# Sorting the tokens of two groups by expert through memory in a four-layer cross-attention kernel

## The chip, the cores and the metric

One core of one Trainium2 chip runs the kernel. The metric is device time in microseconds of one execution, as the median over runs. The engines are TensorE (PE, with its weight loads PEld), VectorE (DVE), ScalarE (ACT), GpSimd (POOL) and SyncE (SP, which here only issues transfers). Every engine takes its own instructions in the order of its own program; the engines wait for each other by semaphores. ACT and POOL can issue transfers too. All data is fp32 but for masks.

## The reference

x is 16 sequences of 56 tokens with 256 channels, the context 16 x 1500 rows of 128. Four layers follow each other, each with attention to the context:

```python
x = _L0_xattn_ref(x, ctx_1024, ...)                  # one head, gate, norm
x = _L1_xattn_ref(x, ctx_1024, mask_BxS2_bk0, ...)   # 16 heads, then feed-forward
x = _L2_xattn_ref(x, ctx_1024, mask_BxS_ik0, ...)    # self, cross, two experts
x = _L3_xattn_ref(x, ctx_1024, mask_BxS2_bk0, ...)   # as L1
```

The third layer has two sets of weights ("vision" and "language"). A token belongs to the first if its type and the next token's type are 1. The end of that layer, which the change rewrites:

```python
vm = vm.at[:, :-1].set((tt[:, :-1] == 1) & (tt[:, 1:] == 1))
mi = rms_norm(hidden_states, ln_post_attn_w)
v_out = jax.nn.silu(mi @ v_gate) * (mi @ v_up) @ v_down
l_out = jax.nn.silu(mi @ l_gate) * (mi @ l_up) @ l_down
hidden_states = hidden_states + jnp.where(vm, v_out, l_out)
```

Gate and up are 256 x 688, down is 688 x 256.

## The kernel before

The 16 sequences are four groups of G = 4; a group has T = 224 tokens, held as two tiles of TP = 112 rows. `items` lists 16 pieces of work, k = 4 x layer + group. For each k, `program` (L1554) runs the attention of that piece (`att0`, `att13`, `att2`), and between its steps it draws pieces of other work from a generator `beside(k)` (L1580): the closing of the piece before (`post...`, called `follows`), and the preparation of the piece after (`pre...`, called `ahead`). Each `yield` ends one such piece; its number is its weight in us, and `pace` (L451) draws pieces until the weights reach a share for each attention step (`SHARES`, L1265, in the third layer). So PE's program is one interleaved list, and work that is not done when an attention ends is run before the next starts. When `k` runs, `line["closed"]` counts the attentions that are closed; a closing waits for it.

*First layer.* `load_pair(n)` (L630) loads the contexts of sequences 2n and 2n+1, and for n > 0 loads the first of the two also turned (channels on partitions), through SP. `turn_pair(n)` (L655) turns the other one by 12 products with the identity (L661), and copies the results from PSUM on ACT and DVE (L666). `scores_pair` (L676) starts after that, by a dependency on the last of these products.

*Second and fourth layer.* `pre13` makes queries, `att13` runs the attention in the short form (only the last 384 context rows count here; a test at the start, L1650 to L1663, finds from the mask which of two programs runs), and `post13` (L992) makes the output product with Wo, the sum, a layer norm, and the feed-forward with W1 and W2. Four weights of 1 MB each go through three buffers (`wpool`, tag w).

*Third layer.* `pre2` (L1133) is norm, self-attention and queries. `att2` (L1462) runs 24 pairs of context blocks for a group: `largest` (L1306, products L1315, maxima L1320 on DVE), `weights_pair` (L1344, products L1352 and L1361, exponentials L1366 on ACT, and running sums `all` on POOL, L1378), `sums_chunk` (L1383, L1391), `keys` and `values` for the sequences ahead (L1286, L1298), `own_sums` (L1409). Weights `pw` have three buffers. `close_group` (L1427) ends a group: product L1435, sum, and `begin_norm` (L326), which scales the rows on POOL (L332).

`post2(gi)` (L1508) is the part quoted of the reference. Each group runs both experts over all of its 224 tokens: the normed rows are turned (`rmsnorm_T`, L337; `to_T`, L264, product L270), and multiplied by the channel weights and by the mask vm or its complement (L360), so that a token of the other expert is a row of zeros. For each expert 6 slices of gate and up, each 2 x 2 products (L1524), then tanh form of silu on ACT, DVE and POOL (L1534), 12 products with down (L1542) and a sum into x (L1548). So a block is 24 + 12 products over 224 tokens, and there are 8 blocks. Each loads its weights through SP.

Of the kernel before, what the change touches and what calls it, by code (L numbers as in the profile page):

```python
# [9 lines left out]
F32 = mybir.dt.float32  # L10
# [12 lines left out]
G = 4  # L23
# [39 lines left out]
def tile_kernel(ctx: ExitStack, tc: tile.TileContext, a, layers=4, groups=NG):  # L63
# [13 lines left out]
    small = ctx.enter_context(tc.tile_pool(name="small", bufs=10))  # L77
    ps_s = ctx.enter_context(tc.tile_pool(name="ps_s", bufs=7, space=PSUM))
    ps_o = ctx.enter_context(tc.tile_pool(name="ps_o", bufs=1, space=PSUM))

# [125 lines left out]
    nc.vector.memset(half_less, -0.5)  # L206
    ones = const.tile([B, 1], F32, name="ones")
    nc.vector.memset(ones, 1.0)
    vm = const.tile([128, B, N], BF16, name="vm")
    nvm = const.tile([128, B, N], BF16, name="nvm")  # L210
    rope = const.tile([TP, 32], F32, name="rope")

    consts = {}

    def load_constants():

        w = wpool.tile([128, 2048], F32, tag="w", name="room")
        consts["room"] = w
        nc.sync.dma_start(w[:, : B * N].bitcast(I32), a["token_types"].to_broadcast([128, B * N]))
        nc.sync.dma_start(  # L220
            w[:N, B * N : B * N + N].bitcast(I32), a["positions"].to_broadcast([N, N])
        )
        nc.sync.dma_start(w[:PR, 1408 : 1408 + N], a["causal"])

    def fill_constants():
# [31 lines left out]
        )  # L257
        nc.vector.tensor_copy(rope, rp[:TP, :32])


# [64 lines left out]

    def begin_norm(w, gi):  # L326

        x = xs[gi]
        rstd = rms_rstd(x, nc.gpsimd)
        xn = xpool.tile([TP, NT, D], F32, tag="xn", bufs=3, name="xn")  # L330
        for i in range(NT):
            nc.gpsimd.tensor_scalar(  # L332
                xn[:, i, :], x[:, i, :], rstd[:, i : i + 1], None, ALU.mult
            )
        begun[w, gi] = xn

# [293 lines left out]
    def load_pair(n):  # L630
# [8 lines left out]
        for b, queue in ((2 * n, nc.sync), (2 * n + 1, other)):  # L639
# [10 lines left out]
            kvs.append(kv[:CP])  # L650
        if n:
            nc.sync.dma_start(kts[0], a["ctxT"][2 * n])
        halves_of[n] = kts, kvs

    def turn_pair(n):  # L655
        kts, kvs = halves_of[n]
        for s in range(NS):
            for i in range(1 if n else 0, 2):
                t = turn()
                for j in range(4):  # L660
                    last = nc.tensor.transpose(  # L661
                        t[:, j * CP : (j + 1) * CP], kvs[i][:, 4 * s + j, :], ident[:CP, :CP]
                    )
                dst = kts[i][:, s * SW : (s + 1) * SW]
                if (i + s) % 2:
                    nc.vector.tensor_copy(dst, t[:, :SW])  # L666
                else:
                    scalar_copy(dst, t[:, :SW])
        halves_of[n] = kts, kvs, last.ins.name

# [5 lines left out]
    def scores_pair(n):  # L676
# [7 lines left out]
        for s in range(NS):  # L684
            sc = psum(ps_s, "sc")
            cols = slice(s * SW, (s + 1) * SW)
            for i in range(2):
                product = nc.tensor.matmul(
                    sc[i * 64 : (i + 1) * 64, :SW], qT[:, b0 + i, :], kts[i][:, cols],
                    start=True, stop=True,  # L690
                )

                tc.add_manual_dep(
                    product.ins, turned_at,
                    mybir.DependencyInfo(
                        mybir.DependencyClass.NoSync, mybir.DependencyReason.DATA
                    ),
                    reason="products in halves stand together",
                )
            nc.vector.tensor_scalar(  # L700
# [290 lines left out]

    def post13(name, gi, state, some=range(NT)):  # L992
        x = xs[gi]
        oT = state["oT"]
        gc = GATE[name + "_attn"]
        if "wo" not in state:
            (state["wo"],) = load_w((a[name + "_Wo"], 8, D))
            (state["w1"],) = load_w((a[name + "_W1"], 2, FFI))
        wo, w1 = state["wo"], state["w1"]
        yield  # L1000
# [17 lines left out]

        yield from turned_back([oT[:, :, i * TP : (i + 1) * TP] for i in some], wo, gc)
        if "w2" not in state:  # L1020
            (state["w2"],) = load_w((a[name + "_W2"], 8, D))
        w2 = state["w2"]
        xT = yield from layernorm_T(gi, name + "_ln_ff_g", name + "_ln_ff_b", some)
# [240 lines left out]
    PAIRS = NC // 2  # L1264
    SHARES = 1.9, 2.4, 2.4, 1.5  # L1265

# [160 lines left out]
    def close_group(b):  # L1427

        if b % G == G - 1:
# [10 lines left out]
            line["closed"] += 1  # L1440
            begin_norm("L2_ln_post_attn_w", b // G)

# [19 lines left out]
    def att2(gi, state, then, ends):  # L1462

        for k in range(G):
            b = gi * G + k
            for j in range(PAIRS):
# [6 lines left out]
                weights_pair(b, j)  # L1473
                pace(SHARES[gi], -0.8, 1)
                last, n = (b, 2 * j - 2) if j else (b - 1, NC - 2)
# [31 lines left out]

    def post2(gi, state):  # L1508
        x = xs[gi]
        xf = x.rearrange("p i d -> p (i d)")  # L1510

        wg, wu = (load_w((a[f"L2_v_{w}"], 2, I2))[0] for w in ("gate", "up"))
        xe = yield from rmsnorm_T("L2_ln_post_attn_w", gi, True)
        yield
        for n, e in enumerate("vl"):
            (down,) = load_w((a[f"L2_{e}_down"], NF2, D))
            hT = big.tile([128, 8, T], F32, tag="hT", bufs=2, name="h2T")
            for f in range(NF2):
# [3 lines left out]
                for k, wt in enumerate((wg, wu)):  # L1522
                    for c in range(2):
                        nc.tensor.matmul(  # L1524
                            p[:w, k * T : (k + 1) * T], wt[:, c, cols], xe[n][:, c, :],
                            start=(c == 0), stop=(c == 1),
# [8 lines left out]
                yield 1.6  # L1535
            if e == "v":
                wg, wu = (load_w((a[f"L2_l_{w}"], 2, I2))[0] for w in ("gate", "up"))
            p = mm()
            for i in range(NT):
                for f in range(NF2):  # L1540
# [5 lines left out]
                    if f % 3 == 2 and i + f < NF2:  # L1546
                        yield 1.3
            nc.vector.tensor_add(xf, xf, p[:TP, : NT * D])  # L1548
            yield 1.3

    def program():  # L1554
        line.update(turn=None, sum=None, side=iter(()), rate=1, closed=0, pair=None, due=0.0, share=0.0)
        for kept in (memory_w, halves_of, queries, heads_w, cross, held, begun):
# [3 lines left out]
        for name in ("L1", "L3"):  # L1560
            parts.append(tuple(partial(f, name) for f in (pre13, first13, att13, post13)))
        parts.insert(2, (pre2, first2, att2, post2))
        items = [(*parts[l], gi) for l in range(layers) for gi in range(groups)]
# [16 lines left out]
        def beside(k):  # L1580
# [10 lines left out]
            if k + 1 < groups:  # L1591
                yield next(ahead)
            if k:
                _, _, _, post, gi = items[k - 1]
                follows = post(gi, states.get(k - 1))
            if k > groups:
                for work in ahead:
                    if isinstance(work, tuple):
                        while line["closed"] < k:
                            yield  # L1600
                        for _ in range(work[1]):
                            yield next(follows)
                    else:
                        yield work
            if k:
                while line["closed"] < k:
# [15 lines left out]
            if k + 1 == len(items) and short:  # L1622
                while line["pair"] != ("L3", groups - 1, 0):
                    yield
                yield from ending(k, 0)

        def ending(k, i):

# [3 lines left out]
            nc.sync.dma_start(a["out"][at : at + TP, :], xs[gi][:, i])  # L1632

        run(before(-1))
        first(0)
        for k, (_, _, att, _, gi) in enumerate(items):
            line.update(side=beside(k), share=1.8 if k + 1 == 2 * groups else 0.0)
            att(gi, states[k], partial(first, k + 1), gi == groups - 1)
            if k + 1 < len(items):
                run(line["side"])  # L1640
# [8 lines left out]

    mk = mpool.tile([B, M], U8, tag="own", bufs=1, name="mk")  # L1650
    nc.sync.dma_start(mk, a["mask"])
    lets = few(3)[:B]
    nc.vector.tensor_reduce(lets[:, 0:1], mk[:, : M - LW], AX.X, ALU.max)
    nc.vector.tensor_reduce(lets[:, 1:2], mk[:, M - LW :], AX.X, ALU.max)
    nc.vector.tensor_tensor(lets[:, 2:3], lets[:, 1:2], lets[:, 0:1], ALU.is_gt)
    load_x(0)
    nc.sync.dma_start(tables, a["tables"])
    t = turn()
    nc.tensor.matmul(t[:1, :1], lets[:, 2:3], ones, start=True, stop=True)
    only_last = const.tile([1, 1], I32, name="only_last")  # L1660
    nc.vector.tensor_scalar(only_last, t[:1, :1], float(B), None, ALU.is_equal)
    short = True
# [39 lines left out]
def layout(i):  # L1702
# [3 lines left out]
    def stacked(w):  # L1706
# [19 lines left out]
        ).view(np.uint32),  # L1726
        "mask": i["mask_BxS2_bk0"].view(np.uint8),
        "mask_last": np.ascontiguousarray(i["mask_BxS2_bk0"][:, M - LW :]).view(np.uint32),
# [16 lines left out]
    for l in ("L1", "L3"):  # L1745
# [3 lines left out]
        out[f"{l}_Wv"] = i[f"{l}_xattn_Wkv"][:, H * 64 :]  # L1749
    for w in (  # L1750
        "v_qkv", "l_qkv", "v_dense", "l_dense",
        "v_gate", "v_up", "v_down", "l_gate", "l_up", "l_down",
    ):
        out[f"L2_{w}"] = stacked(i[f"L2_xattn_{w}"])
    ckv = i["L2_xattn_ckv_w"]
    cd = i["L2_xattn_cdense_w"]
# [41 lines left out]
```

## Time and profile before

| what | value |
|---|---|
| three runs | 1456.79, 1458.99, 1459.77 us; median 1458.99 |
| the profiled execution | 1451.74 us, its span 1449.9 us |
| busy PE, DVE, ACT, POOL | 1387.7, 791.7, 742.5, 510.6 us |
| mean granted TensorE clock | 0.988 |
| moved by transfers | 131.08 MB |
| stages by lines: first layer | to about 128 us |
| second, third, fourth layer | to about 434, 1117, 1450 us |

A line of the groups of instructions gives: source line, engine, operation, tile written <- tiles read, shapes and count, then busy time in us, mean ns of one, and the idle time of the engine just before such instructions with what ended it. A line of the waits gives: engine, tile, line <- what released it, then us in total, times, and the longest. Busy digits of the page are tenths in 40 slices of 36 us. A line of transfers gives: target <- source, queue, count, KB of one, and us from issue to landing.

### The profile page before, as it was taken

How to read it: one execution, taken by the hardware profiler on the slowest of the kernel's cores; microseconds unless marked ns; L12 is line 12 of the kernel's file. 1: busy time of each engine (PE TensorE's matmuls, PEld its weight loads, DVE VectorE, ACT ScalarE, POOL GpSimd, SP SyncE). 2: the span in 40 equal slices, each digit the busy share in tenths (PEclk: the TensorE clock that was granted, in tenths of full speed). 3: DMA queues.
4: the chain of work that ended last, by engine and by line, in shares of the span. 5: the costliest groups of instructions: out<-in, count | busy, mean ns of one | idle time of the engine just before them, and what ended most of it. 6: DMA issues, size and time to landing. Idle time of an engine off the chain costs nothing.

```text
span 1449.9 us, 32736 instructions
## 1 busy us (share of the span) xinstructions
PE 1387.7 (96%) x13816; PEld 965.3 (67%) x13816; DVE 791.7 (55%) x1802; ACT 742.5 (51%) x1713; POOL 510.6 (35%) x554
## 2 busy tenths in 40 slices
PE   6999999998998999999999999999999999999997
PEld 4677677775775556655666556666666777777776
DVE  5454755547346574457555575445546546554641
ACT  2334857665353353535444354444545656756661
POOL 0021001010010566676677667767872110000000
PEclk9999999999899999999999999999999999999999
DMA  7823233241231202110112001221103333334230
GB/s 283 316 84 140 66 116 117 89 143 30 90 119 48 80 23 82 58 42 23 64 61 102 23 21 64 84 90 45 46 29 118 112 125 116 123 99 139 89 106 10
DMA packets 34298, 131.08 MB, mean 90 GB/s; under 512 B 8013, under 2 KB 14429, under 8 KB 30045
## 3 DMA queue, kind: packets, MB, share of 16 engines
q1 hardware_dynamic: 32701, 122.59, 24.7%
q0 software_dynamic: 720, 3.93, 0.7%
q8 instruction: 111, 1.82, 0.5%
q10 hardware_dynamic: 720, 2.36, 0.4%
q14 instruction: 46, 0.38, 0.1%
HBM read 127.95 MB, written 0.92 MB: 89 GB/s over the span
## 4 chain that ended last, share of the span: by engine, by line
PE 79%; DVE 10%; ACT 6%; DMA 2%; POOL 1%; issue 1%; SPq 0%; DVEq 0%; ACTq 0%; POOLq 0%
PE sc L562 10%; PE sc L544 8%; PE sc L1009 7%; PE sc L1315 7%; PE sc L1524 5%; PE o L1391 5%; PE sc L1361 4%; PE sc L825 4%; PE sc L1542 3%; PE sc L1298 3%; PE sc L1286 3%; DVE mx L1320 3%; PE sc L1031 3%; PE sc L1352 2%; PE sc L1152 2%; PE sc L897 2%
## 5 line engine op out<-in xcount | busy, mean ns | idle before, releaser
L1378 POOL TENSOR_TENSOR all<-all,pw 125x448 f32<-125x448 f32 x300 | 341.1, 1148 | 132.3 <-ACT pw L1366 121.2
L1320 DVE TENSOR_REDUCE mx<-sc 112x1 f32<-112x500 f32 x384 | 233.3, 668 | 113.1 <-PE sc L1315 113.0
L1366 ACT ACTIVATE pw<-sc 125x448 f32<-125x448 f32 x384 | 177.7, 549 | 95.8 <-PE sc L1361 91.7
L551 ACT ACTIVATE p<-p,few 128x384 f32<-128x384 f32 x224 | 136.9, 612 | 88.1 <-DVE few L547 87.8
L544 PE MATMUL sc<-ktl,qa 128*128 128x384 f32 x448 | 177.8, 505 | 0.0
L547 DVE CUSTOM_DVE_ANT_0 p<-sc,mkl 128x384 f32<-128x384 f32 x224 | 121.6, 551 | 87.2 <-PE sc L544 81.6
L562 PE MATMUL sc<-p,kvl 32*128 32x224 f32 x2160 | 153.1, 356 | 5.1 <-DVE qa L858 3.7
L142 POOL TENSOR_SCALAR mkl<-m32l 128x384 bf16<-128x384 uint8 x32 | 16.4, 513 | 397.3 <-DVE few L547 355.5
L562 PEld LDWEIGHTS sc<-p,kvl 32*128 32x128 f32 x2160 | 138.8, 187 | 21.1 <-issue 8.5
L562 PE MATMUL o<-p,kvl 32*128 32x224 f32 x720 | 146.3, 355 | 0.0
L562 PEld LDWEIGHTS o<-p,kvl 32*128 32x128 f32 x720 | 132.4, 187 | 0.0
L1315 PE MATMUL sc<-ck,qs 32*112 32x500 f32 x768 | 129.0, 624 | 3.1 <-ACT ck L262 1.4
L262 ACT ACTIVATE p<-p,few 128x384 f32<-128x384 f32 x224 | 120.7, 611 | 5.9 <-DVE few L538 5.9
L581 DVE STREAM_TRANSPOSE p<-p 128x768 f32<-128x768 f32 (+1 forms) x96 | 102.6, 1094 | 17.6 <-ACT p L262 17.1
L544 PEld LDWEIGHTS sc<-ktl,qa 128*128 128x128 f32 x448 | 78.9, 191 | 36.2 <-issue 8.2
L262 ACT ACTIVATE ot<-sc 128x224 f32<-128x224 f32 x64 | 31.9, 606 | 137.1 <-PE o L562 87.8
L1361 PE MATMUL sc<-qs,ck 32*125 32x224 f32 x1536 | 93.9, 349 | 0.0
L1391 PEld LDWEIGHTS o<-pw,vc 125*32 125x32 f32 x1536 | 40.1, 109 | 80.5 <-issue 68.8
L1391 PE MATMUL o<-pw,vc 125*32 125x224 f32 x1536 | 92.6, 359 | 0.0
L279 POOL TENSOR_TENSOR stat<-stat,half_less 112x2 f32<-112x2 f32 (+1 forms) x33 | 23.0, 699 | 183.7 <-DVE stat L292 143.8
L1524 PE MATMUL sc<-xT,w 128*128 128x224 f32 (+1 forms) x384 | 82.5, 359 | 0.0
L938 DVE COPY ot<-sc 128x224 f32<-128x224 f32 x32 | 18.2, 570 | 110.9 <-PE o L562 97.3
(265 smaller groups left out, 2419.0 us busy)
## 6 DMA issues: line engine op xcount, KB each, us to landing
kvl<-in_ctx_last SPq DMA_DIRECT2D x30, 768.0 KB, 4.3
kt<-in_ctxT SPq DMA_DIRECT2D x23, 750.0 KB, 5.0
w<-in_L_W SPq DMA_DIRECT2D x16, 1024.0 KB, 4.9
w<-in_L_Wq SPq DMA_DIRECT2D x8, 1024.0 KB, 4.9
w<-in_L_Wo SPq DMA_DIRECT2D x8, 1024.0 KB, 4.8
ktl<-in_ctxT SPq DMA_DIRECT2D x32, 192.0 KB, 2.5
w<-in_L_v_qkv SPq DMA_DIRECT2D x4, 768.0 KB, 4.5
w<-in_L_l_qkv SPq DMA_DIRECT2D x4, 768.0 KB, 4.4
```

Of the source, the lines that this page charges most:

```text
L262: nc.scalar.activation(out, in_, AF.Copy, scale=scale)
L544: nc.tensor.matmul(sc[:, :LW], u["q"][:, i * 128 : (i + 1) * 128], u["kt"], start=True, stop=True)
L547: nc.vector.tensor_tensor_reduce(u["p"][:, i], sc[:, :LW], u["mask"], 1.0, -LOWEST, ALU.add, ALU.min, mn[:, i : i + 1],)
L551: nc.scalar.activation(u["p"][:, i], u["p"][:, i], AF.Exp, bias=mn[:, i : i + 1], scale=-1.0, accum_out=den[:, i : i + 1],)
L562: product = nc.tensor.matmul(o[g][:, : RB * BW], y["kv"][part, j, :], y["p"][part, :, j * BW : (j + 1) * BW], start=j == 0, stop=j == LB - ...
L1315: nc.tensor.matmul(banks[g][: 2 * N, :SW], made["q"][part, rows], made["k"][part, cols], start=True, stop=True,)
L1320: nc.vector.tensor_reduce(made["mx"][:, half * 4 + g, s : s + 1], banks[g][: 2 * N, :SW], AX.X, ALU.max)
L1361: nc.tensor.matmul(banks[g][:CP, c * QH : (c + 1) * QH], made["k"][part, at : at + CP], made["q"][part], start=False, stop=c == 1, skip_gr ...
L1366: nc.scalar.activation(p[:, :, g * QH : (g + 1) * QH], banks[g][:CP, : 2 * QH].rearrange("p (c n) -> p c n", c=2), AF.Exp,)
L1378: engine.tensor_tensor(made["all"][:, cols], made["all"][:, cols] if j else p[:, 0, cols], p[:, c, cols], ALU.add,)
L1391: nc.tensor.matmul(made["o"][part, :QH], made["v"][:, n, part], p[:, r * QH : (r + 1) * QH], start=n == 0, stop=n + 1 == NC, skip_group_ch ...
L1524: nc.tensor.matmul(p[:w, k * T : (k + 1) * T], wt[:, c, cols], xe[n][:, c, :], start=(c == 0), stop=(c == 1),)
```

## The change

The change has four parts.

1. *The closing of the third layer by pairs of groups.* `post2(pair)` handles two groups (448 tokens) as 3 blocks of 224 rows. `begin_norm(..., sort=True)` writes each scaled row by an indirect transfer, issued by POOL, to a row buffer in DRAM (`sorted_rows`, 672 rows, filled with zeros early on); the row's place comes from a running count: vision tokens from the front, the others from the back. Block v takes the vision weights, block l the language weights, and the middle block b those of the one of the two that has more than 224 tokens; its weights are gathered by an indirect transfer with an index for each partition (`choice`). Results go to a second buffer (`made_rows`) through ACT's queue, and come back by an indirect gather for each half of a group (`back`).
2. *Closings held back.* `post13` of the second layer's groups 2 and 3 pauses before its feed-forward, and goes on beside the third layer's groups 0 and 1 (`late`). Pair 0 is closed beside groups 2 and 3 of the third layer, pair 1 beside the fourth layer's group 0. Shares change.
3. *Contexts of sequence pairs 4 to 7* are both loaded turned; `turn_pair` does nothing for them.
4. *The test of the mask* runs on 128 partitions instead of 16.

```diff
+    dpool = ctx.enter_context(tc.tile_pool(name="rows", bufs=1, space=bass.MemoryType.DRAM))
...
+        cp = mm()
+        nc.tensor.matmul(cp[:TP, :8], first[:, :TP], is_v, start=True, stop=False)
+        nc.tensor.matmul(cp[:TP, :8], every[:, :TP], carry, start=False, stop=True)
+        nc.vector.tensor_add(index, cp[:TP, :8], less)
+        nc.vector.tensor_copy(place[:TP], index)
...
-    def begin_norm(w, gi):
+    def begin_norm(w, gi, sort=False):
...
-        begun[w, gi] = xn
+            if sort:
+                nc.gpsimd.indirect_dma_start(
+                    sorted_rows[gi // 2], bass.IndirectOffsetOnAxis(place_of(gi, i), 0),
+                    xn[:, i, :], None,
+                )
+        if not sort:
+            begun[w, gi] = xn
...
-        if n:
-            nc.sync.dma_start(kts[0], a["ctxT"][2 * n])
+        for i in range(0 if n == 0 else 1 if n < 4 else 2):
+            nc.sync.dma_start(kts[i], a["ctxT"][2 * n + i])
...
-            for i in range(1 if n else 0, 2):
+            for i in range(0 if n == 0 else 1 if n < 4 else 2, 2):
...
+        while pause and pause():
+            yield
...
-    SHARES = 1.9, 2.4, 2.4, 1.5
+    SHARES = (2.3, 1.5), (2.3, 0.8), (2.3, 1.7), (1.65, 1.65)
...
-    def post2(gi, state):
+    def post2(pair):
+        def weights(e, name, c, f):
+            if e != "b":
+                return load_w((a[f"L2_{name}"][128 * "vl".index(e) :][:128], c, f))[0]
+            w = wpool.tile([128, 2048], F32, tag="w", name="w")[:, : c * f]
+            nc.gpsimd.indirect_dma_start(
+                w, None, a[f"L2_{name}"],
+                bass.IndirectOffsetOnAxis(choice[:, pair : pair + 1], 0),
+            )
+            return w.rearrange("p (c f) -> p c f", c=c)
+        def rows_of(n):
+            rows = tmp("rows")[:TP].rearrange("p (i d) -> p i d", i=NT)
+            nc.sync.dma_start(
+                rows,
+                sorted_rows[pair][n * T : (n + 1) * T].rearrange("(i p) d -> p i d", p=TP),
+            )
+            return rows
...
-        for n, e in enumerate("vl"):
-            (down,) = load_w((a[f"L2_{e}_down"], NF2, D))
+        for n, e in enumerate("vbl"):
+            p = to_T(rows)
...
+            down = weights(e, "down", NF2, D)
...
-            if e == "v":
-                wg, wu = (load_w((a[f"L2_l_{w}"], 2, I2))[0] for w in ("gate", "up"))
+            if n < 2:
+                wg, wu = (weights("vbl"[n + 1], w, 2, I2) for w in ("gate", "up"))
+                rows = rows_of(n + 1)
...
-            nc.vector.tensor_add(xf, xf, p[:TP, : NT * D])
+            y = tmp("made")[:TP]
+            scalar_copy(y, p[:TP, : NT * D])
+            nc.scalar.dma_start(
+                made_rows[pair][n * T : (n + 1) * T].rearrange("(i p) d -> p i d", p=TP),
+                y.rearrange("p (i d) -> p i d", i=NT),
+            )
...
+        for gi in (2 * pair, 2 * pair + 1):
+            y = tmp("back")[:TP]
+            back.append((xs[gi].rearrange("p i d -> p (i d)"), y))
+            for i in range(NT):
+                nc.gpsimd.indirect_dma_start(
+                    y[:, i * D : (i + 1) * D], None, made_rows[pair],
+                    bass.IndirectOffsetOnAxis(place_of(gi, i), 0),
+                )
...
+        for xf, y in back:
+            nc.vector.tensor_add(xf, xf, y)
...
+            third = 2 * groups - 1 <= k < 3 * groups
...
+                if third:
+                    follows = line["late"]
+                elif k == 3 * groups:
+                    follows = post2(1)
...
+        def late():
+            third = 2 * groups
+            def at(k):
+                return line["k"] > k or line["k"] == k and (line["behind"] or line["beside"])
+            for gi in (groups - 2, groups - 1):
+                while line["closed"] < groups + gi + 1:
+                    yield
+                yield from post13(
+                    "L1", gi, states[groups + gi],
+                    pause=lambda: not at(third if gi == groups - 2 else third + 1),
+                )
+                begin_norm("L2_ln_in_w", gi)
+                line["stage"] += 1
+            while line["closed"] < third + 2 or not at(third + 2):
+                yield
+            yield from post2(0)
+            begin_layernorm("L3_ln_q_g", 0)
...
-            line.update(side=beside(k), share=1.8 if k + 1 == 2 * groups else 0.0)
+                side=beside(k), share={2 * groups - 1: 1.4, 3 * groups: 2.4}.get(k, 0.0), k=k, behind=0, beside=0,
```

## The prediction

> **What bounds the kernel now.** I read the page's slices first, then the groups of TensorE (PE), then windows, waits and transfers.
>
> ```profile
> PE   6999999998998999999999999999999999999997
> POOL 0021001010010566676677667767872110000000
> PE 79%; DVE 10%; ACT 6%; DMA 2%; POOL 1%; issue 1%; SPq 0%; DVEq 0%; ACTq 0%; POOLq 0%
> 616.00:652.00 36.00, 36.00 (x357) 18.97 (x355) 20.66 (x39) 14.60 (x31) 25.99 (x24) 1.00 0.12 42
> ```
>
> PE is busy nearly everywhere (1387.7 of 1449.9 us) and carries 79% of the chain that ended last. The last line is a stretch of the third layer (start:end, length, busy us of PE, weight loads, DVE, ACT, POOL, then clock and DMA): PE 36.00 of 36, POOL 26. So whatever PE instruction leaves this stage shortens it by its full time, and POOL (GpSimd) has 10 us free in 36.
>
> ```profile
> L1524 PE MATMUL sc<-xT,w 128*128 128x224 f32 (+1 forms) x384 | 82.5, 359 | 0.0
> L1542 PE MATMUL sc<-w,h2T 128*112 128x256 f32 x192 | 51.1, 394 | 0.0
> L270 PE MATMUL sc<-ident,xn 112*128 112x112 f32 x112 | 16.7, 269 | 5.4 <-DVE xn L296 5.4
> L661 PE MATMUL sc<-ident,kv__504 125*128 125x125 f32 x12 | 1.7, 274 | 0.0
> L661 PE MATMUL sc<-ident,kv__596 125*128 125x125 f32 x12 | 1.4, 270 | 0.0
> L661 PE MATMUL sc<-ident,kv__830 125*128 125x125 f32 x12 | 1.4, 270 | 0.0
> ```
>
> These are the groups that the change cuts. The number after the bar is busy time with overlaps counted once, so it, and not the 359 ns of one record, is the price. An fp32 product shows as two records: 384 are 192 products.
>
> ```profile
> 350.00:360.00 10.00, 6.09 (x81) 3.73 (x83) 9.42 (x25) 7.66 (x20) 0.00 (x0) 0.84 0.03 3
> 360.00:370.00 10.00, 10.00 (x142) 8.20 (x140) 2.79 (x6) 1.48 (x4) 0.00 (x0) 0.64 0.02 3
> 400.00:410.00 10.00, 6.54 (x20) 4.34 (x19) 5.11 (x18) 4.66 (x14) 5.53 (x9) 0.73 0.56 193
> PE sc L270 <- DVE xn L296: 5.4, 2, 2.9
> PE sc L1099 <- DVE stat L1090: 3.8, 1, 3.8
> ```
>
> The one region where PE stands is the end of the second layer: two gaps of 3.9 and 3.5 us, each beside a lower granted clock (0.84 and 0.64; 0.73). A gap costs about twice its length: 3.9 idle plus (0.36 + 0.16) x 10 of clock. The waits name them: a norm's rows (L296), and the softmax sums of the first self-attention (L1090).
>
> **The change part by part.** Built, the changed program has 144 gate/up and 72 down products where there were 192 and 96.
>
> *Fewer blocks.* Per pair of groups 3 blocks of 224 rows replace 4; two blocks go. Gate/up: 48 x 82.5/192 = 20.6 us. Down: 24 x 51.1/96 = 12.8. Each block turns its own rows, 24 transposes for 16: 8 x 16.7/112 = +1.2. Net -32.2 us, all on PE in stages where PE is full.
>
> *Contexts 4 to 7 loaded turned.* 48 transposes go: 1.7 + 1.4 + 1.4 of the rows shown, 1.4 for the fourth (inside kv), -5.9 us. Their 12 evictions leave ACT and DVE. Added: four 750 KB loads on SP; the zero fill of the two row buffers adds 1.4 MB. That is 4.4 MB, 11 us at the 411 GB/s of 40 to 50 us. The cover is the DMA share of 0.35, 0.62, 0.12, 0.17, 0.54, 0.13 from 70 to 130 us. Where they are issued sooner, they meet 1.01. Bounds 0 to +6 (half the transfer); I take +2, since pairs 4 to 7 are used after 70 us.
>
> *Start.* Two reductions of 1.30 and 0.53 us become 140 and 48 wide: by those two rows 1.05 ns an element and 0.13 fixed, 0.45 together; a cast and a count are added. -1 us. The sort's constants are 3 tiny products (0.27 each by L255) behind some 25 DVE instructions of 0.06 to 0.2: 0 to 4, taken +1.
>
> *Closings held back.* The feed-forward of group 2 leaves the end of the second layer and runs among the third's attention pairs. The 400 us gap is its norm, which PE reaches at once; now work stands between. In the built order an attention sum (4.8 us of products) also stands between the second self-attention scores and the first turned weights, where none stood. Removing one gap with its clock is -7, both -15; both moved elsewhere 0, a new one +4. I take -6.
>
> *The way through memory* adds waits. The nearest rows:
>
> ```profile
> L649 POOL DMA_DIRECT2D kv<-in_ctx x2 | 1.3, 658 | 39.2 <-DMA kt<-in_ctxT 31.6 <-PE o L753 7.6
> kv<-in_ctx POOLq DMA_DIRECT2D x2, 768.0 KB, 6.6
> w<-in_L_l_up SPq DMA_DIRECT2D x4, 688.0 KB, 5.7
> out_x<-x SPq DMA_DIRECT2D x2, 112.0 KB, 2.6
> L332 POOL TENSOR_SCALAR xn<-x,stat 112x256 f32<-112x256 f32 x24 | 22.0, 928 | 1.0
> ```
>
> No indirect transfer is in the trace. Lower bound of an issue on POOL: the direct one's 0.66 us; upper: 6.6, if POOL were held until landing. I take 0.7, the same instruction kind. 22 are added (8 scatters, 6 weight gathers, 8 returns); 12 multiplications of 0.66 us leave POOL. Queued behind them there are the sums of weights (4 x 1.15 us per attention pair). Three buffers of weights let PE go on for three pairs, some 18 us, so an issue plus the second scatter's wait for the first to land (2.6) is covered: 0. Without that cover it would be 3 to 4 us at each of four closings.
>
> Three hand-overs stand in PE's own order:
> (a) *Pair 0's return.* After its last down product: copy 0.6 (512-wide evictions on ACT), write 2.6 to 5.2 (outputs of 112 and 224 KB), four gathers issued 2.6, landing 2.5 (192 KB into ktl), two sums 1.4 (L1548), statistics 1.3, root 0.7 (L279), scaling 2.4 (L296, twice 1225 ns): 14.1 to 16.7 us. In front of the turned rows PE has three attention pairs by their starts near 941 us, 3 x (1.17 + 1.04 + 0.89), two value steps of 1.07, sums of 0.5: 12.0. Late by 2 to 5; 0 to +10 with clock, taken +5. Behind it waits the fourth layer's first query.
> (b) *Pair 1's rows.* By the times of before: close at 1117.5, first scaled rows 1121.5, scatter 0.6 + 2.6, second 0.6 + 2.6, reload 0.3 + 2.5: 1130.7. PE gets there after the same work as before (1130.75) less one score (0.65): 1130.1. 0 to +6, taken +1. SP waits meanwhile; behind stands the first down weight, not used for 12 us.
> (c) *Block b's weights.* Gathered once the last gate/up product is done and POOL's last multiplication past (0.37 + 0.39 on ACT, 0.39 DVE, 0.66 POOL: 1.8 us), issue 0.7, landing 5.7 to 6.6: 8.2 to 9.1. PE has 12 down products, four scores, a turn: 5.6 + 2.6 + 0.4 = 8.6. 0 to +5, taken +1.
>
> Copies and stores on ACT (6 x 1 us) and sorting's row traffic lie beside PE: ACT is 51% busy.
>
> Two pages of the Trainium skill speak against this. "DMA: Bandwidth & Descriptors", section "Anatomy of one DMA", puts most of about 2 us fixed cost of a transfer into the receipt of the write, worst in HBM; by its fit a scatter of 112 KB would be an estimated 2.3 us. The 2.6 of the output's row agrees; by the page (b) would be just in time and the sum 1 us lower. "TensorE: Matmul & The Clock Gate", Part 1, says that an idle window of about 3.4 us drops the array to half clock. The 0.64 after the 3.9 us gap agrees; by it (a), if under 3.4, would cost only its length.
>
> **Sum.** -32.2 - 5.9 - 1 = -39.1; +2 +1 +5 +1 +1 = +10; held back -6; rounded with what the many small waits of a new order may add (+2): -33 us. The profiled execution took 1451.74 (span 1449.9), so 1419; its like among the runs shown, median 1458.99, lies 7 us higher, and the changed kernel's runs should too: 1426.
>
> **Rivals.**
> *Full gain, 1409.* No new wait shows and the gaps go: -39 - 11. For: PE's order leaves 8 to 12 us for each hand-over. Against: all three sums end within 5 us of it.
> *Half gain, 1444.* All upper bounds of (a) to (c) and layer one: +27 for +9, so -15. For: PE takes its instructions in order, so one late row stops attention too. Against: every row there would have to be at its slow end.
> *Slower: an indirect issue holds POOL.* Place: eight issues before PE's own waits, four in (a), two each in (b) and (c). If each holds POOL h us, PE loses 8 x (h - 0.7) and some 4 of clock at each of three gaps. Without (a) to (c) the change is worth -40; it is slower from 8 x (h - 0.7) = 31, h = 4.6. At h = 6: -40 + 42 + 12 = +14, 1473. For: no row of this trace prices an issue whose addresses are data. Against: five direct issues of 128 rows took 0.55 to 0.77.
> *It doesn't do what it says.* Excluded by the counts of built products.
>
> **How the numbers follow.** Forecast 0.46 (own range 1414 to 1437), half gain 0.22, full 0.17, slower 0.12, no change 0.03: faster 0.85. Below 0.2% (3 us) nothing could be told apart. Range: from 1406 to 1450, which leaves out the slower cases and the far end of the full gain.
>
> **What would show it.** The gate/up and down groups at 62 and 38 us; transposes of contexts about 9; no PE wait over 3 us on rows, gathered weights or the fourth layer's first norm; POOL's indirect issues near 0.7 us; the clock whole from 350 to 430. PE busy near 1350. It is wrong if busy time falls by 38 and the span does not: then the idle time in front of those three places is the answer; or if the gaps of the second layer only move.

## The result and the profile after

The changed kernel is slower: 1469.41 us (four runs, 1466.75 to 1470.86) against 1458.09 for the kernel before on the same chip, a ratio of 1.0087 with a 95% interval of 1.0059 to 1.0115: 11 us more by the medians, some 13 by the ratio. The forecast of 1426 us has the wrong sign, and the time lies outside its range.

The page of the changed kernel, its head and the busy tenths and clock of TensorE (PE) in 40 slices:

```profile
span 1465.8 us, 32406 instructions
PE 1376.5 (94%) x13638; PEld 950.6 (65%) x13638; DVE 781.4 (53%) x1796; ACT 742.6 (51%) x1695; POOL 522.8 (36%) x564
PE   7989999999899999999999999999899959999997
PEclk9999999999999999999999999999799979999998
```

The span grew by 15.9 us although PE does less. PE's busy time fell by 11.2 us (from 1387.7) and not by the 38 of the forecast, and two holes are new: a slice near 1040 us with a low clock and one near 1190 where PE is half idle.

The groups of instructions of the changed kernel: what it removes is removed as forecast.

```profile
L1605 PE MATMUL sc<-xT,w 128*128 128x224 f32 (+1 forms) x288 | 61.7, 362 | 0.8 <-DVE xT L1593 0.6 <-ACT made L302 0.2
L1624 PE MATMUL sc<-w,h2T 128*112 128x256 f32 x144 | 38.3, 396 | 0.0
L1371 PE MATMUL sc<-ck,qs 32*112 32x500 f32 x768 | 138.3, 623 | 3.2 <-ACT ck L302 1.4 <-issue 0.7 <-DVE mx L1376 0.7
L376 POOL DMA_INDIRECT sorted<-xn,place x8 | 8.1, 1011 | 11.1 <-DMA sorted<-xn,place 7.9 <-issue 2.5 <-POOL xn L372 0.7
L1644 POOL DMA_INDIRECT back<-made,place x8 | 7.6, 952 | 8.3 <-DMA made<-made 6.4 <-issue 1.8
```

Gate/up cost 61.7 us and down 38.3, as the prediction said (62 and 38). An indirect issue holds POOL for 1.0 us. But the scores of the third layer's cross attention (L1371), which the change does not touch, cost 138.3 us where the same 768 records cost 129.0 before:

```profile
L1315 PE MATMUL sc<-ck,qs 32*112 32x500 f32 x768 | 129.0, 624 | 3.1 <-ACT ck L262 1.4 <-issue 0.7 <-DVE mx L1320 0.7
```

Stages show where the time went. The borders are the first scores of the second layer (L544 before, L593 after), the first scores of the third layer's cross attention and its last products with values. (The attention of the second and fourth layer is the short form, `att13`, over the last 384 context rows; the expectations below call it self-attention.) First the kernel before, then the changed one (columns as in the prediction's window lines):

```profile
0.00:123.00 123.00, 105.93 (x869) 79.93 (x869) 59.27 (x167) 40.63 (x81) 13.14 (x22) 0.97 0.62 223
123.00:436.50 313.50, 296.23 (x2767) 226.04 (x2766) 173.02 (x450) 193.36 (x471) 27.56 (x45) 0.97 0.30 98
436.50:1113.10 676.60, 662.14 (x7225) 403.27 (x7225) 389.10 (x743) 310.61 (x688) 442.03 (x445) 1.00 0.16 56
1113.10:1449.90 336.80, 323.36 (x2964) 256.09 (x2962) 170.34 (x443) 197.85 (x474) 27.85 (x42) 0.99 0.31 103
```

```profile
0.00:125.10 125.10, 106.58 (x826) 79.30 (x827) 54.83 (x181) 38.54 (x77) 13.20 (x22) 0.96 0.71 256
125.10:416.70 291.60, 278.12 (x2695) 210.78 (x2695) 169.28 (x440) 185.61 (x463) 26.77 (x44) 0.98 0.30 99
416.70:1088.30 671.60, 647.00 (x7077) 388.34 (x7077) 381.67 (x723) 312.74 (x667) 442.17 (x441) 0.98 0.16 54
1088.30:1465.80 377.50, 344.77 (x3043) 272.15 (x3042) 175.60 (x453) 205.70 (x489) 40.66 (x57) 0.96 0.31 102
```

The first layer is 2.1 us longer. The second is 21.9 shorter, of which some 16 are the feed-forward of group 2 (by the starts of its records on PE), which now runs in the third. The third does three blocks less (3 x 16.7 = 50 us at the prediction's prices) and that feed-forward more; it should be some 34 us shorter and is only 5.0. The fourth does one block more (17 us) and is 40.7 longer. So the third layer lost 29 us and the fourth 24. Part of it is the clock, which these rows give as 1.00 and then 0.98 in the third layer and 0.99 and then 0.96 in the fourth: an estimate of 10 to 13 us in each (the difference times the length).

The waits of PE and of DVE (VectorE) in the changed kernel name two of the causes:

```profile
PE sc L310 <- POOL xn L336: 16.1, 2, 15.4
PE sc L1408 <- DVE mx L1376: 12.2, 4, 7.2
DVE x L1651 <- DMA back<-made,place: 13.6, 4, 5.1
```

The longest of the first line is the return of pair 1 in the fourth layer. Its way through memory in POOL's time order (start, length, instruction, idle time before it):

```profile
1182.28 0.51 POOL L143 TENSOR_SCALAR mkl<-m32l 128x384 bf16<-128x384 uint8 x1 [6.85 <-issue]
1188.06 0.99 POOL L1644 DMA_INDIRECT back<-made,place  x1 [5.26 <-DMA made<-made]
...
1191.84 0.93 POOL L1644 DMA_INDIRECT back<-made,place  x1 [0.31 <-issue]
1197.30 0.72 POOL L319 TENSOR_TENSOR stat<-stat,half_less 112x2 f32<-112x2 f32 x1 [4.52 <-DVE stat L332]
1198.13 2.44 POOL L336 TENSOR_SCALAR xn<-x,stat 112x256 f32<-112x256 f32 x2
```

PE's last down product starts near 1180. POOL waits for the written rows until 1188.06, issues four gathers until 1192.8, DVE waits for them and sums, and PE has the first normed rows at 1199.4: 19 us, in which PE stands 15.4. DVE stands at the sums meanwhile, with the softmax of the fourth layer's attention behind them.

The third cause is in no wait of PE's own line. Two attention pairs of the changed kernel that follow each other, in PE's time order:

```profile
744.18 0.93 PE L1417 MATMUL sc<-qs,ck 32*125 32x224 f32 x16
744.94 2.40 PE L1371 MATMUL sc<-ck,qs 32*112 32x500 f32 x8
747.27 0.96 PE L1447 MATMUL o<-pw,vc 125*32 125x224 f32 x16
...
749.50 0.93 PE L1417 MATMUL sc<-qs,ck 32*125 32x224 f32 x16
750.36 1.98 PE L1061 MATMUL sc<-w,hT 128*112 128x256 f32 x8
752.27 1.11 PE L1371 MATMUL sc<-ck,qs 32*112 32x500 f32 x8
...
755.58 0.95 PE L1417 MATMUL sc<-qs,ck 32*125 32x224 f32 x16
```

The first pair has no side work and takes 5.32 us (744.18 to 749.50); its eight score records take 2.40. The second has 1.98 us of side work (L1061) and takes 6.08; its eight records take 1.11. So 1.98 us of side work cost 0.76 here, and PE counts as busy throughout. What the scores wait for was to be seen in the kernel before, in the waits of its weight loads, which the prediction does not show:

```profile
PEld sc L1315 <- ACT pw L1366: 15.9, 49, 1.2
```

These scores read nothing that the exponentials (L1366) write. What is left for them to wait for is the PSUM bank (the memory that products write to) that the exponentials empty: a pair draws four banks for weights, four for scores and one for keys or values from a ring of seven. Experiment e13 tests this.

### The profile page after: what moved, and what is told of

Read it like the earlier page. It is cut to its first block, busy times and chain, and to the rows that moved or that the text cites. A ratio compares the mean times of both kernels' runs of the same rounds, so it can differ in the third digit from the quotient of the medians.

```text
span 1465.8 us, 32406 instructions
## 1 busy us (share of the span) xinstructions
PE 1376.5 (94%) x13638; PEld 950.6 (65%) x13638; DVE 781.4 (53%) x1796; ACT 742.6 (51%) x1695; POOL 522.8 (36%) x564
## 4 chain that ended last, share of the span: by engine, by line
PE 75%; DVE 12%; ACT 7%; DMA 4%; issue 1%; POOL 1%; SPq 0%; POOLq 0%; DVEq 0%; ACTq 0%
PE sc L611 10%; PE sc L593 8%; PE sc L1371 7%; PE sc L1061 7%; PE o L1447 5%; PE sc L1417 4%; PE sc L1605 4%; PE sc L876 3%; DVE mx L1376 3%; PE sc L1354 3%; PE sc L1342 3%; PE sc L1408 3%; ACT p L302 2%; PE sc L1087 2%; PE sc L1624 2%; PE sc L1208 2%
## 5 line engine op out<-in xcount | busy, mean ns | idle before, releaser
L593 PE MATMUL sc<-ktl,qa 128*128 128x384 f32 x448 | 177.3, 505 | 0.0
L611 PEld LDWEIGHTS sc<-p,kvl 32*128 32x128 f32 x2160 | 138.3, 187 | 20.7 <-issue 8.6
L1371 PE MATMUL sc<-ck,qs 32*112 32x500 f32 x768 | 138.3, 623 | 3.2 <-ACT ck L302 1.4
L593 PEld LDWEIGHTS sc<-ktl,qa 128*128 128x128 f32 x448 | 78.9, 191 | 36.7 <-issue 8.7
L1417 PE MATMUL sc<-qs,ck 32*125 32x224 f32 x1536 | 97.8, 358 | 0.0
L1417 PEld LDWEIGHTS sc<-qs,ck 32*125 32x125 f32 x1536 | 77.8, 186 | 1.2
L302 ACT ACTIVATE ck<-sc 128x500 f32<-128x500 f32 x48 | 28.2, 588 | 92.6 <-PE sc L1342 92.6
```

Source lines behind the costliest of these rows:

```text
L302: nc.scalar.activation(out, in_, AF.Copy, scale=scale)
L593: nc.tensor.matmul(sc[:, :LW], u["q"][:, i * 128 : (i + 1) * 128], u["kt"], start=True, stop=True)
L611: product = nc.tensor.matmul(o[g][:, : RB * BW], y["kv"][part, j, :], y["p"][part, :, j * BW : (j + 1) * BW], start=j == 0, stop=j == LB - ...
L1371: nc.tensor.matmul(banks[g][: 2 * N, :SW], made["q"][part, rows], made["k"][part, cols], start=True, stop=True,)
L1417: nc.tensor.matmul(banks[g][:CP, c * QH : (c + 1) * QH], made["k"][part, at : at + CP], made["q"][part], start=False, stop=c == 1, skip_gr ...
```

## The experiments

The theories: (A) both returns from memory are hand-overs without cover; (D) the third layer's PE is not full, its waits for banks count as busy time, and side work fills them; (F) the first layer's transposes stood in a wait. The rivals stand in the expectations.

Stage lengths in us from the profiled executions, and ratios to the kernel before with 95% intervals:

| kernel | first | second | third | fourth | ratio |
|---|---|---|---|---|---|
| before | 123.0 | 313.5 | 676.6 | 336.8 | 1 |
| changed | 125.1 | 291.6 | 671.6 | 377.5 | 1.0087 (1.0059 to 1.0115) |
| e1 query later | 124.6 | 291.0 | 672.3 | 372.6 | 1.0056 (1.0034 to 1.0077) |
| e2 pair 0's query later | 123.8 | 290.1 | 674.1 | 374.7 | 1.0058 (1.0037 to 1.0079) |
| e3 sums behind scores | 124.2 | 289.8 | 670.3 | 357.9 | 0.9933 (0.9913 to 0.9954) |
| e11 pair 1 only | 124.3 | 291.1 | 672.3 | 359.6 | 0.9935 (0.9914 to 0.9956) |
| e4 sums between | 124.5 | 291.6 | 718.2 | 374.6 | 1.0346 (1.0307 to 1.0384) |
| e6 turned on PE | 125.9 | 291.0 | 677.8 | 381.2 | 1.0077 (1.0053 to 1.0101) |
| e7 no block b, pair 0 | 124.2 | 291.1 | 662.0 | 363.3 | 0.9902 (0.9885 to 0.9919) |
| e12 no block b, pair 1 | 125.9 | 291.1 | 667.8 | 343.8 | 0.9806 (0.9783 to 0.9828) |
| e8 keys first, on e3 | 120.8 | 291.1 | 662.5 | 365.8 | 0.9869 (0.9852 to 0.9885) |
| e9 keys first, on before | 123.3 | 313.7 | 671.9 | 338.1 | 0.9968 (0.9950 to 0.9985) |
| e10 not held back | 125.1 | 313.1 | 660.5 | 359.8 | 0.9993 (0.9975 to 1.0011) |
| e13 six banks | 125.0 | 291.9 | 693.4 | 365.0 | 1.0127 (1.0078 to 1.0176) |

A stage of one execution moves by some us with no change to it. The first layer is one and the same program in the changed kernel and all its versions but e6, and took 120.8 to 125.9 us; the third is the same in the changed kernel, e1, e6 and e11 and took 671.6 to 677.8; the fourth is the same in e3, e7, e8, e10 and e11 and took 357.9 to 365.8. So a difference of 5 to 8 us between two stages shows little by itself.

### The returns: e1, e2, e3, e11

**e1.** Before the preparation of group 2 in the fourth layer:

```diff
+            if k == 3 * groups + 1:
+                for _ in range(12):
+                    yield
```

> Only the first query rows of group 2 in the fourth layer are asked for 12 side steps later; the sums of pair 1's return stay where they are on DVE. Theory A (the return of pair 1 is a hand-over that nothing covers: 15.4 us of PE idle and a clock of 0.70 and 0.88 in two windows of 20 us): PE meets its own scores in the gap, the wait on xn goes, but DVE still stands some 6 us in front of the sums with the softmax behind it, so a wait of 3 to 6 us stays: about 1453 us (1449 to 1458). Rival B (the end of the fourth layer is set by something else and a gap only moves): 1466 to 1471.

Measured: 1463.6 us, above A's range (1449 to 1458) and below B's (1466 to 1471). The 15.4 us wait is gone, but others came: 7.5 us at 1200 and 3.2 at 1247, both on DVE.

```profile
PE sc L898 <- DVE ot L989: 7.5, 1, 7.5
PE sc L1087 <- DVE xT L351: 4.4, 3, 3.2
```

So giving PE something to do is not enough while the sums stand at the head of DVE.

**e2.** More steps before the sums of pair 0 (six for two). In the built order the query rows moved two pairs later on PE; the sums did not move on DVE.

> Four more side steps between the gathers of pair 0's return and its norm: the fourth layer's first query rows come two attention pairs later on PE, while the sums keep their place in DVE's order. Theory A (the 7.2 us that PE stands near 1041 us come from DVE: the two sums stand at its head and wait 5.1 and 2.1 us for the returned rows, with the maxima of the scores behind them): nothing changes, 1466 to 1471, and PE's wait on the maxima stays at 6 to 8 us. Rival C (the query rows come too early, as hand-over (a) of the prediction has it): the gap goes, 1457 to 1461.

Measured: 1465.24 us, ratio 1.0058 (1.0037 to 1.0079), and PE's wait on the maxima stays at 7.0 us. The time is just under A's range, but the wait that C wanted gone is there: DVE holds PE, not the query rows.

**e3.** The sums follow the newest scores on DVE, by an order without a semaphore: pair 0's after six steps instead of two, pair 1's nine steps into the next attention, then eight more to its query rows.

```diff
+    def add_back():
+        after = line["dve"]
+        for xf, y in line.pop("back"):
+            added = nc.vector.tensor_add(xf, xf, y).ins
+            tc.add_manual_dep(added, after, ...)
...
+                add_back()
+                begin_layernorm("L3_ln_q_g", 2)
+                for _ in range(8):
+                    yield
```

> The sums of both returns are put behind the newest scores on DVE by an order without a semaphore, and both query rows come later on PE. Theory A (both gaps come from the way back through memory): 7.2 and 15.4 us of idle and some 8 us of cold clock go: about 1441 us (1437 to 1447), no PE wait over 3 us after 1000 us. Rival B (a gap only moves): 1455 or more, with a new wait of 7 us or more in the fourth layer.

Measured: 1446.25 us, in A's range. No PE wait over 3 us is left after 1000 us, and the fourth layer is 19.6 us shorter than in the changed kernel. This version is 0.7% faster than the kernel before.

**e11.** Of e3, only the half of pair 1.

> Of the two returns only pair 1's has its sums behind the scores and its query rows later; pair 0's is as in the changed kernel. Theory A with the sizes of the traces: pair 1's return is some 19 us, pair 0's mostly moved (the 7.2 us wait gave way to waits of 2.9, 2.0 and 1.9 us): 1447 to 1452, and PE waits 7 us on the maxima near 1045 us. Rival (both count alike): 1455 to 1460.

Measured: 1448.65 us, in A's range, ratio as in e3. So taking away the wait for pair 1's return is worth 1.5% (22 us by the ratios; 18.5 between the two profiled executions, 1465.8 and 1447.3), and pair 0's cannot be told from nothing: in e3 its 7.2 us wait gave way to waits of 2.9, 2.0 and 1.9 us, the first behind DVE's bookkeeping, the others behind POOL's sums of weights.

### What PE's busy time holds: e4, e13, e8, e9

**e4.**

```diff
                 weights_pair(b, j)
+                last, n = (b, 2 * j - 2) if j else (b - 1, NC - 2)
+                if last >= 0:
+                    sums_chunk(last, n)
+                    sums_chunk(last, n + 1)
                 pace(SHARES[gi][line["behind"]], -0.8, 1)
-                last, n = (b, 2 * j - 2) if j else (b - 1, NC - 2)
...
-                if last >= 0:
-                    sums_chunk(last, n)
-                    sums_chunk(last, n + 1)
```

> In the third layer the products of weights with values (two chunks, 0.96 us) are moved from behind the scores of the next batch to in front of them. Theory D (PE is not full there: the scores wait for PSUM banks that ACT has yet to empty, and the profile shows this wait as longer products, 2.15 us for eight instead of 1.11, 12 times in the changed kernel and 5 times in the one before): the scores' line falls from 138 to about 128 us and the kernel by 8 to 12 us, 1457 to 1461. Rival E (PE is full, a product takes what its group shows): 1467 to 1471 and the line stays at 138.

Measured: 1508.59 us, outside both. The groups of e4:

```profile
L1371 PE MATMUL sc<-ck,qs 32*112 32x500 f32 x768 | 114.3, 628 | 2.8 <-ACT ck L302 1.4 <-issue 0.7 <-DVE mx L1376 0.7
L1417 PE MATMUL sc<-qs,ck 32*125 32x224 f32 x1536 | 113.0, 371 | 0.0
L1408 PE MATMUL sc<-shift,ones_r 2*125 2x448 f32 x384 | 95.7, 473 | 30.3 <-DVE mx L1376 17.1 <-DVE gated L1612 5.2 <-ACT l L302 1.3
```

The scores fell by 24 us, more than D said, but the next weights (L1408, L1417) rose from 58.3 and 97.8 to 95.7 and 113.0. My reading, which this run does not show by itself: scores that start later give their banks back later, so the wait moved and grew. No product was added, yet PE's busy time is 1400.5 us for 1376.5; part of that is a colder clock (0.97 in the third layer for 0.98, over 718 us). E, which had the scores' line stay, is refuted, and so is D's hope of a gain from this order.

**e13.** The ring of banks: `bufs=6` for `bufs=7`, on e3.

> The version with the sums behind the scores (1446 us), with six PSUM banks in the ring of scores, weights and side work instead of seven; nothing else differs. Theory D (in the third layer PE waits for banks, 9 of which a pair takes from the ring, and the wait is booked as busy time): the third layer, 670 us with seven, gets at least 0.5 us longer for each of its 64 pairs, so 700 us or more, and the busy time of PE in it grows with no product added. Rival I (the waits there come from data, the exponentials or the maxima, and not from banks): the third layer stays within 10 us of 670.

Measured: 1475.25 us (two runs). The third layer of e3, then of e13:

```profile
414.00:1084.30 670.30, 646.04 (x7077) 387.91 (x7077) 382.96 (x723) 312.80 (x667) 443.05 (x441) 0.99 0.16 54
```

```profile
416.90:1110.30 693.40, 676.21 (x7077) 403.78 (x7077) 382.15 (x723) 313.35 (x667) 443.25 (x441) 0.99 0.15 52
```

The same 7077 records at the same granted clock (0.99), 23.1 us longer, and PE is busy 30.2 us more. The time lies between the two ranges (D: 700 or more, I: 660 to 680). A group has 24 pairs, so there are 96 and not the 64 that the expectation counts: 0.24 us a pair, half of the 0.5 that it named. The weight loads of the scores that wait for the exponentials grew from 20.1 us in e3 to:

```profile
PEld sc L1371 <- ACT pw L1422: 35.2, 108, 2.0
```

So a bank less makes the scores wait for exponentials that they don't read, and the wait is booked as work of PE. With seven banks the same line has 46 such waits in e3, 49 in the kernel before.

**e8** (on e3) and **e9** (on the kernel before): `values` and `keys` of a later batch stand directly behind `pace`, in front of the scores.

> On the version with the sums behind the scores (1446 us), the keys or values of a later batch (1.1 us of products, one PSUM bank) are moved from behind the scores to in front of them, so that they and not a wait stand between the weights and the scores of a pair. Theory D: the scores' products fall from about 132 to 110 us, the weights keep theirs because the maxima on DVE still have the products with values (0.96 us) to run beside, and the kernel gains 8 to 20 us: 1426 to 1438. Rival H (the banks go round in order, so the wait only moves to the weights as it did where the products with values were moved, which cost 39 us): 1446 to 1480.

> The same move made in the kernel before the change. Theory D: its pairs have side work more evenly (5 groups of scores directly behind the weights where the changed kernel has 12), so the gain is smaller: 4 to 12 us, 1446 to 1454. Rival H: 1456 or slower.

Measured: e8 1438.64 us, just above what D said; e9 1452.42, in D's range. Putting 1.1 us of other products in front of the scores gains 7.6 and 4.5 us. D's mechanism came half true: the scores of e8 fell from 137.3 to 120.7 us and not to 110, and the weights, which D had keep theirs, rose from 57.4 and 97.3 to 68.8 and 102.3. So most of the wait moved to the weights, as H said, and a part went. e8 is the fastest complete version; like against like (e8 to e9) the change with its returns mended is worth about 14 us.

### What a block and a stage are worth: e7, e12, e10, e6

**e7** and **e12** leave out the same block, once beside the third layer's cross attention (pair 0), once beside the fourth layer's attention (pair 1). The cut shows the one line for e7; the loads, and the rows of the block, follow from it.

```diff
-        for n, e in enumerate("vbl"):
+        for n, e in ((0, "v"), (1, "b"), (2, "l")) if pair else ((0, "v"), (2, "l")):
```

> On the version with the sums behind the scores (1446 us), block b of pair 0 is left out: 24 gate/up and 12 down products, 4 transposes, its weights and its evictions; the rows made by block v are written twice in its stead, so the rows of block b get those of block v. Theory D (beside attention a product of side work hides part of PE's waits for PSUM banks: a pair with none takes 5.3 us, one with 1.98 us of it 6.1): by that ratio, 0.77 for 1.98, the 16 us of the block are worth 5 to 8 us: 1438 to 1441. Rival E (PE is full in the third layer, as the prediction had it): all 16 to 17 us go, 1429 to 1431.

> On the version with the sums behind the scores (1446 us), block b of pair 1 is left out instead of pair 0's, so the same products in the fourth layer; its rows get those of block v. If side work is worth its full time beside the self-attention of the fourth layer (no longer products for want of a bank there): 16 to 18 us less, 1428 to 1431. If waits there take it up as in the third layer: 1440 to 1443.

Measured: e7 1442.24 us, 4 less than e3 and just outside D's range; e12 1428.99, 17 less and in the range of full worth. Stage by stage the third layer of e7 is 8.3 us shorter, of a block of 16 to 17, and its scores' line rose from 137.3 to 146.8. Not all of that rise is waits for banks: beside a wait of 2.2 us for the exponentials at 990 us the granted clock of e7 was 0.69, 0.50 and 0.55 in the stretches to 995, 1000 and 1010 us, and its third layer has 0.98 where e3 has 0.99. (Its fourth layer is 5.4 longer, at a clock of 0.98 for 0.99, which makes some 3.6 of it by an estimate, 0.01 of 360 us; all of it is within the spread of that stage.) The fourth layer of e12 is 14.1 shorter. So the same products are worth a quarter (by the whole times) to half (by the stage) in the third layer and nearly all in the fourth.

**e10** runs the feed-forward of group 2 at the end of the second layer again, with the share of side work from before, on e3.

> On the version with the sums behind the scores (1446 us), the feed-forward of group 2 runs at the end of the second layer again, with the share of side work that it had there before the change. Theory D: its 16 us of PE work are paid in full there, with the gaps of that stage (some 4 us more of idle and the clock beside them), and give back only a quarter in the third layer (4 us of 16, as block b did): 12 to 18 us slower, 1458 to 1464. Rival E (PE full in both stages, so only the gaps count, the 6 us of the prediction): 1449 to 1453.

Measured: 1456.34 us, between the two. By stages: the second layer 23.3 us longer, its 3.8 and 2.9 us gaps back; the third 9.8 shorter. So holding back is worth some 9 us by the ratios, more than E had it, and the 16 us of work cost 10 in the third layer, not the 4 of D.

**e6** undoes the turned loads in the changed kernel: one more context of each pair is turned on PE.

> The changed kernel with contexts 4 to 7 turned on PE again, as before the change (part 3 alone undone). Theory F (these transposes stood in waits of the first layer, so taking them away bought a wait of 2.8 us for the exponentials at 85 us and a cold clock behind it): the first self-attention scores start at 123 to 126 us as in the changed kernel (125.1) and the time stays at 1466 to 1471; the 2.8 us wait goes and the context transposes show some 15 us again. Rival G (4.7 us of PE work were saved there, and something else in the first layer got slower): scores at 129 to 130 us, 1472 to 1475.

Measured: 1470.25 us, the first scores of the second layer at 125.9 us, both as F said. In the changed kernel PE waits 2.8 us at 85, where transposes stood before; the weight load there waits for a copy of turned weights on DVE (L798), not for exponentials, as the expectation has it. In e6 the wait is gone (PE 10.00 busy of 10 us from 80 on, clock 1.00) and the context transposes show 15.9 us for 10.3. These 5.5 us of PE work change the stage by 0.8, less than it moves by itself, and the two times cannot be told apart.

## Why the prediction was wrong, point by point

*"So whatever PE instruction leaves this stage shortens it by its full time."* This sentence failed, and the -32.2 with it. PE 36.00 of 36 was read as full; part of what is booked as busy in that stage is waiting for banks (e13). At the prices of e7 and e12, three blocks out of the third layer are worth 3 x 4 = 12 us (whole times) to 3 x 8.3 = 25 (stage), and one more in the fourth costs 14 to 17: between -11 and +5 in place of -32. The counts and the group prices (62 and 38) were right; what was wrong is that a group's busy time is its worth. The Trainium skill has the warning, in "Perfetto Trace Analysis", section "Identifying the Most-Contended Engine": the busy share of TensorE does not tell how near it is to its limit. It explains this by pipelined instructions that look smaller than they are; here they look larger (676.2 us of busy time in e13 for the 7077 records that take 646.0 in e3).

*"Three hand-overs stand in PE's own order."* There were four. Pair 1's return in front of the fourth layer's query rows of group 2 was not in the list, and by e11 it is the largest term of all: 18.5 to 22 us. Its chain had been worked out for pair 0 (14.1 to 16.7 us) and was 2 to 5 us short of the 19 measured: the four gathers took 4.7 us to issue and not 2.6, the last write 5.9 and not 2.6 to 5.2. I did not ask where the second return ends.

*(a) Pair 0's return, +5.* A wait came (7.2 us, in a window of 20 us at a clock of 0.61), but not where I put it. I counted PE's work in front of the query rows; the sums at the head of DVE, with the maxima behind them, held PE earlier. I named what is queued behind POOL's issues and not behind DVE's sums. What it cost in the end stays open: taking it away gained nothing that can be measured (e3 against e11).

*(b) and (c).* In their ranges: PE waited 2.0 us on the sorted rows and not at all on gathered weights.

*Contexts turned, -5.9 +2; start, 0 in sum.* PE saved 5.0 us (15.3 of transposes before, 10.3 after) and the kernel nothing that can be told (e6). I asked what the added transfers would meet, not what the removed transposes stood in. The first layer is 2.1 us longer than before, which is within its spread; the start and the constants were not tried apart.

*Closings held back, -6.* Right in kind; 9 by e10. The gaps of the second layer went.

*The slower rival.* Its sign came true, its mechanism did not: an indirect issue holds POOL for 1.0 us, not 4.6.

Put together: -11 to +5 for the blocks, +18.5 to +22 for the fourth hand-over, -9 for holding back and 0 to +2 for the first layer make -2 to +20. The 13 us measured lie in that, so the two failed steps are large enough to account for the miss; how it splits between them, and what pair 0's return adds, is not settled to some us.

## What to carry to other kernels

A full busy line of PE is no proof that PE is the bound: look at a repeated loop with and without side work, and at the waits of the weight loads, before pricing what leaves it. The same block was worth 4 us of the whole time in one stage and 17 in another. For every value that goes through memory, list each place where it comes back, and for each engine on its way what stands behind the instruction that waits: a sum of 0.7 us at the head of DVE held PE for 7 us.

## What the runs showed of the hardware

- Waits for PSUM banks show as busy time of PE: six banks for seven added 30 us of it to one stage, with the same records and the same granted clock (e13).
- An indirect issue took POOL 1.0 us in the mean (1011 and 952 ns above); direct ones of 128 rows had taken 0.54 to 0.77. A write of 224 KB from ACT's queue, which the returns wait for, landed in 5.0 us at the median, 2.6 at the shortest and 5.9 at the longest.
- A short wait can take clock with it. After the wait of 2.8 us at 85 us the granted clock of the changed kernel was (window, its length, busy times, then clock):

```profile
84.00:86.00 2.00, 1.01 (x12) 1.01 (x14) 1.75 (x8) 0.96 (x1) 0.10 (x1) 0.84 0.86 244
86.00:90.00 4.00, 4.00 (x44) 3.62 (x42) 0.51 (x2) 0.67 (x2) 3.20 (x4) 0.65 0.69 234
```

The Trainium skill, "TensorE: Matmul & The Clock Gate", Part 1, names one idle window of about 3.4 us as what lowers the clock. Here a wait of 2.8 us was followed by a clock of 0.84 and 0.65, and the measurement decides. By these rows some 1.7 us of clock (0.16 x 2 + 0.35 x 4) go beside the wait; that it cost the kernel time is not shown, since e6, without the wait and the dip, ended its first layer no sooner.
